# Layer 2 of a two-layer selective-scan kernel: the first group's preparation written as one ordered list, with x_proj of the second and third group moved into the first group

## The chip, the cores and the metric

The kernel runs on one core of a Trainium2 chip, as one launch. The metric is the device time of that launch in microseconds. Five engines work side by side, each with its own instruction queue that it takes in order: TensorE (PE), VectorE (DVE), ScalarE (ACT), GpSimd (POOL), and SyncE (SP), which here only issues DMAs. Semaphores make one engine wait for another. [...]

## What is computed

Two layers, each a residual block on a 64 x 64 image with 96 channels: group norm, an input projection to 192 channels and a gate, a 3 x 3 depthwise convolution with SiLU, four directional state-space scans, a layer norm, the gate, and an output projection. The change is in the scans of the second layer:

```python
xs = jnp.stack([xf, xf[:, :, ::-1], xf[:, :, o1], xf[:, :, o2]], axis=1)
x_dbl = jnp.einsum('bkdl,kcd->bkcl', xs, x_proj_weight)          # x_proj
dts = jnp.einsum('bkrl,kdr->bkdl', x_dbl[:, :, :DT_RANK], dt_projs_weight)
Bs = x_dbl[:, :, DT_RANK:DT_RANK + D_STATE]
Cs = x_dbl[:, :, DT_RANK + D_STATE:]
A = -jnp.exp(A_logs)
# selective_scan, for each of the 4096 positions t:
delta = softplus(dts + dt_projs_bias)
h = h * exp(delta_t * A) + (delta_t * u_t) * B_t                 # 192 channels x 16 states
y = sum over states of h * C_t                                   # + u * D
```

## The kernel before

**Groups and units.** Layer 2's scans (function `scans`, lines 654 to 1040) are cut into 16 groups: two kinds of path, two directions each, four chunks of 1024 positions (`TC`) each. The 192 channels are three tiles T of 64; the two halves of the 128 partitions hold an even and an odd state, so that 16 states are 8 pairs m (`NP`). One unit is one (T, m): a tile of 128 partitions by 1024 positions. A group has 24 units (`PER`), the whole layer 384. The order within a group goes by twos: T = 0 with m = 0 and 1, T = 1 with m = 0 and 1, T = 2, then m = 2 and 3, and so on.

**What one unit does.** `stage_a`: ACT makes the decay a = exp(dt * A). The input b comes in two ways. For an even unit, `stage_B` has PE spread the row of B over the partitions (bank pair b0), and DVE multiplies it by du in `stage_b`. For an odd unit, ACT has made products bT of the transposed du and a column of B (`product`), and `stage_t` has PE transpose eight of them into bank pair b1; no DVE multiplication is needed. `stage_s`: DVE's scan h = a * h + b, which needs the end of the previous group's scan of that unit (`carry`). `stage_c`: POOL multiplies h by C (tile cb, fetched from DRAM by `fetch_c` on SP's queue, three buffers). `stage_r`: PE folds the two states and adds into the banks y0, y1, y2; the first unit of a T begins its bank with a matmul of y. PSUM has eight banks: b0 and b1 two each, y0 to y2, and one named v.

**The preparation of a group** (`prelude`, from line 714). `project` has PE compute x_proj (pj) in two halves of 512 positions, three matmuls each; `projected` copies it to xd (one buffer) on ACT. `first_part`, `less_part`, `next_part` split B into three bfloat16 pieces: ACT casts a piece, PE subtracts it in pj (weights `less`), ACT casts the next, and so twice. `rows` writes C to DRAM. `tokens_B` transposes B on PE, `tokens_B_out` copies it to BT on ACT. `delta(T)` is softplus with a correction for what is lost in 1 + w: PE computes pd (`begin`); ACT does Abs, Relu, Exp, Ln and Identity; DVE does the `missed` step (w); and three two-operand steps (ln, sp, su: `found`, `whole`, `times`) follow on POOL, or on DVE for group 0. `spread(T)` copies sp to dt and su to du, onto both partition halves, by eight DMAs on SP's queue. `tokens_du` transposes su on PE, `tokens_du_out` copies it to duT on ACT. Sixteen `product` operations on ACT then make the bT of two m.

**What sets the order.** Each step of a preparation has a slot, counted in units from the start of the previous group, so that a group is prepared while the one before it scans. A main loop over j issues one round of stages for unit j and then the steps whose slots have come. Steps with a slot below 0 (all of group 0's preparation, and x_proj and the first pd of group 1) are issued before the loop. Up to j = 0 a scheduler may move instructions within a queue; from j = 0 on every instruction is held in program order, by these lines:

```python
def issue(*args, **more):
    ins = op(*args, **more)
    return tc.keep_in_program_order(ins) if pinned else ins
```

All instructions issued through this class have one line number in the profile, 670, and are told apart by their tiles. Group 0's preparation uses the banks y0, y1 for pj and y2, b1, v for pd; every later group uses v for everything.

Of the kernel before, what the change touches and what calls it, by code (L numbers as in the profile page):

```python
# [8 lines left out]
F32 = mybir.dt.float32  # L9
# [34 lines left out]
def two_ss2d_layers(  # L44
# [609 lines left out]
    def scans(weights):  # L654
# [2 lines left out]


        xw, dwb, _ = weights
        pinned = []  # L660

        class Ordered:
            def __init__(self, engine):
                self.engine = engine
# [1 line left out]
            def __getattr__(self, name):  # L666
                op = getattr(self.engine, name)

                def issue(*args, **more):
                    ins = op(*args, **more)  # L670
                    return tc.keep_in_program_order(ins) if pinned else ins

                return issue

        pe, act, dve, pool, sp = (
            Ordered(e) for e in (nc.tensor, nc.scalar, nc.vector, nc.gpsimd, nc.sync)
# [1 line left out]
        with ExitStack() as sc:  # L678
# [2 lines left out]
            pps = sc.enter_context(tc.tile_pool(name="pps", bufs=1, space=PSUM))  # L681
            dram = sc.enter_context(tc.tile_pool(name="dram", bufs=3, space=DRAM))
            load_exp_ln()
            am = decays(weights[2])
            carry = pre.tile([128, 3, NP], F32, name="carry")
            PER = 3 * NP
            LAG = 3
# [6 lines left out]
            def spare(name, tag="v"):  # L694

                if tag[0] == "b":
                    return pps.tile([128, TC], F32, tag=tag, name=name)[:, 0:HT]
                return pps.tile([128, HT], F32, tag=tag, name=name)
# [12 lines left out]
            def chunk(t, c):  # L711
                return t[:, HT * c : HT * (c + 1)]

            def prelude(k):


                p, d, c = GROUPS[k]
                me = state[k]
                add_engine = pool if k else dve

                tags = ("y0", "y1", "y2", "b1", "v") if k == 0 else ("v",) * 5

# [39 lines left out]

                def tokens_B():

                    ps = me["ps"] = spare(f"tB{k}")
                    for q in range(8):
                        pe.transpose(
                            ps[:, 32 * q : 32 * (q + 1)],
                            xd[0:32, 128 * q : 128 * (q + 1)], ident[0:32, 0:32],
                        )  # L770
# [8 lines left out]

                def tokens_du(e):  # L780

                    ps = me["ps"] = spare(f"tu{k}_{e}")
                    for T in range(3):
                        pe.transpose(
                            ps[:, 128 * T : 128 * (T + 1)],
                            me["su", T][:, 128 * e : 128 * (e + 1)], ident,
                        )

                def tokens_du_out(e):
                    t = me["duT", e] = pre.tile(  # L790
                        [128, 2, 3, 64], F32, tag=f"duT{e}", name=f"duT{k}_{e}"
                    )
                    act.copy(t, me["ps"][:, 0:384].rearrange("p (b h c) -> p h b c", h=2, c=64))


                def delta(T):

                    def begin():
                        ps = me["pd", T] = spare(f"pd{k}_{T}", tags[2 + T])
                        for h, half in enumerate(HALF):  # L800
                            pe.matmul(
                                ps[half], dwb[p][96 : NC + 1, d, T, half],
                                xd[96 : NC + 1, halves[h]], start=True, stop=True,
                            )

                    def new(nm, own):
                        t = me[nm, T] = pre.tile(
                            [128, HT], F32, tag=f"{nm}{T}" if own else nm, name=f"{nm}{k}_{T}"
                        )
                        return t  # L810

                    def absolute():
                        act.activation(new("su", True), me["pd", T], AF.Abs)

                    def positive():
                        act.activation(new("sp", True), me["pd", T], AF.Relu)

                    def exponent():
                        act.activation(new("w", False), me["su", T], AF.Exp, scale=-1.0)

                    def logarithm():
                        act.activation(new("ln", False), me["w", T], AF.Ln, bias=one)

                    def plus():
                        act.activation(me["pd", T], me["w", T], AF.Identity, bias=one)

                    def missed():

                        dve.scalar_tensor_tensor(
                            me["w", T], me.pop(("pd", T)), -1.0, me["w", T], ALU.add, ALU.subtract  # L830
                        )

                    def found():
                        add_engine.tensor_sub(me["ln", T], me["ln", T], me["w", T])

                    def whole():
                        add_engine.tensor_add(me["sp", T], me["sp", T], me["ln", T])

                    def times():
                        add_engine.tensor_mul(me["su", T], me["sp", T], chunk(u[T], c))  # L840

                    return [
                        begin, absolute, positive, exponent, logarithm, plus, missed,
                        found, whole, times,
                    ]

                def spread(T):
                    for nm, of in (("dt", "sp"), ("du", "su")):
                        t = me[nm, T] = pre.tile(
                            [128, TC], F32, tag=f"{nm}{T}", name=f"{nm}{k}_{T}"  # L850
                        )
                        both(t.rearrange("p (h t) -> p h t", h=2), me[of, T], sp)

                steps = []
                if (p, d) == (1, 0):
                    steps += [(-17 + T, lambda T=T: turn(T)) for T in range(3)]
                for h in range(2):
                    o = -13 + 3 * h

                    late = 0 if k else 9.5  # L860
                    steps += [
                        (o, lambda h=h: project(h)),
                        (o + 1, lambda h=h: projected(h)),
                        (o + 1 + late, lambda h=h: first_part(h)),
                        (o + 1 + late, lambda h=h: less_part(h)),
                        (o + 2 + late, lambda h=h: next_part(0, h)),
                        (o + 2 + late, lambda h=h: less_part(h)),
                        (o + 3 + late, lambda h=h: next_part(1, h)),
                    ]
                steps += [  # L870
                    (-9, rows), (-6.8, tokens_B), (-5.95, tokens_B_out),

                    *zip((-1.5, -1, -1, 0, 1, 1, 2, 3, 4, 5), delta(0)),
                    *zip((2.5, 3, 3, 4, 5, 5, 6, 7, 8, 9), delta(1)),
                    *zip((6.5, 7, 7, 8, 9, 9, 10, 11, 12, 13), delta(2)),
                ]
                steps += [(18.5 + e, lambda e=e: tokens_du(e)) for e in range(4)]
                steps += [(19 + e, lambda e=e: tokens_du_out(e)) for e in range(4)]
                steps += [(18 + 2 * T, lambda T=T: spread(T)) for T in range(3)]


                turns = (
                    (19, (4, 4, 4, 4)), (PER, (3, 1, 5, 1, 3, 3)), (PER + 6, (4, 2, 3, 1, 3, 3)),
                    (PER + 12, (2, 3, 3, 2, 3, 3)),
                )
                for i, (slot, counts) in enumerate(turns):
                    todo = [(e, h, n) for e in range(4) for h in range(2) for n in range(2)]
                    for s, count in enumerate(counts):
                        steps += [
                            (slot + s + 0.1, lambda i=i, at=at: product(k, i, *at))  # L890
                            for at in todo[:count]
                        ]
                        del todo[:count]
                return steps

            def product(k, i, e, h, n):


                me = state[k]
                if (h, n) == (0, 0):  # L900
                    me["bT", i, e] = mn.tile(
                        [128, 2, 3, 2, 64], F32, tag="bT", name=f"bT{k}_{i}{e}", bufs=7
                    )
                q = 2 * (2 * i + 1) + n
                act.mul(
                    me["bT", i, e][:, h, :, n, :], me["duT", e][:, h],
                    me["BT"][:, e + 4 * h, q : q + 1],
                )
# [90 lines left out]
            def stage_y(j):  # L999
# [6 lines left out]
                        act.copy(view, f(ps))  # L1006

            steps = [
                (PER * (k - 1) + slot, n, step, k)
                for k in range(len(GROUPS)) for n, (slot, step) in enumerate(prelude(k))  # L1010
            ]

            steps.sort(key=lambda at: (at[0] >= 0, at[0] < 0 and at[3], at[:2]))
            while steps[0][0] < 0:
                steps.pop(0)[2]()

            def unit(step, at):
                if 0 <= at < N:
                    step(at)

            for j in range(-5, N + LAG + 2):
                if j == 0:
                    pinned.append(True)

                for ahead, odd in ((4, 0), (1, 1)):
                    k, i = divmod(j + ahead, PER)
# [353 lines left out]
```

## Time and profile before

| | us |
|---|---|
| median of 3 runs | 1559.88 (1557.27 to 1559.94) |
| profiled execution, time | 1555.25 |
| its span, first to last instruction | 1553.5 |
| busy: PE / DVE / ACT / POOL | 1256.0 / 1350.1 / 1203.1 / 1093.8 |
| x_proj of layer 2's group 0 begins | 288.96 |
| first scan of group 0 / first DVE multiplication of group 1 | 314.31 / 412.51 |
| one scan of 128 x 1024 (xcount 288 and 96) | 2.34 and 2.28 |
| one DVE multiplication of 128 x 1024 | 1.21 |
| mean granted TensorE clock over the span | 0.91 |

Times in the profile are microseconds from the span's start. A row of a timeline gives the start, the duration, the engine, the line, the operation, the tile written and the tiles read (buffer numbers left out), the shapes, and how many such instructions are merged into the row; in brackets stands how long the engine was idle before it and whose instruction ended that. "PE b" means that a matmul that writes tile b was the last to come. Clock 0.50 is half of TensorE's full clock. A PE row counts the two passes of a 32-bit matmul as two instructions. The time of a run is a little longer than the span, 1555.25 against 1553.5.

### The profile page before, as it was taken

The page shows a single profiled execution, that of the slowest core. Times are in us where ns is not written, and L with a number is a line of the kernel's source. Part 1 is how long each engine was busy: PE and PEld are TensorE (multiplying, and loading weights), DVE is VectorE, ACT ScalarE, POOL GpSimd, SP SyncE. Part 2 cuts the span into 40 slices and gives each one's busy share as a digit, 9 for nine tenths or more (in the row PEclk, how much of TensorE's full clock was granted, in tenths as well). Part 3 has the DMA queues.
Part 4 walks back from the last instruction along what each step waited for, and adds up shares of the span by engine and source line. Part 5 has one row for each costly group of instructions (what it writes and reads, how often), then busy time and mean ns, then how long its engine had stood idle before and what let it go on. Part 6 is the DMA issues. An engine that isn't in the chain of part 4 may idle for free.

```text
span 1553.5 us, 17352 instructions
## 1 busy us (share of the span) xinstructions
PE 1256.0 (81%) x5158; PEld 504.4 (32%) x5158; DVE 1350.1 (87%) x932; ACT 1203.1 (77%) x2476; POOL 1093.8 (70%) x577
## 2 busy tenths in 40 slices
PE   5954779769888979887888889797978888876778
PEld 3433424223233323332333333333333332322223
DVE  6836489339999999999999999999999999999976
ACT  3445134759999898989999999999898989987733
POOL 0032000019898989899998989898989999998750
PEclk8975689759999999999989999999999899999999
DMA  4031320432626263544526262526263443626233
GB/s 110 20 107 35 105 71 1 134 73 55 138 57 136 64 145 80 123 100 92 134 68 151 59 138 56 136 57 149 68 138 82 110 110 82 136 62 152 60 93 83
DMA packets 83059, 146.33 MB, mean 94 GB/s; under 512 B 31580, under 2 KB 33820, under 8 KB 82860
## 3 DMA queue, kind: packets, MB, share of 16 engines
q1 hardware_dynamic: 80844, 144.35, 38.4%
q10 hardware_dynamic: 2112, 0.79, 0.2%
q8 instruction: 42, 0.69, 0.2%
q14 instruction: 61, 0.50, 0.1%
HBM read 80.85 MB, written 12.13 MB: 60 GB/s over the span
## 4 chain that ended last, share of the span: by engine, by line
DVE 28%; issue 22%; PE 13%; ACT 10%; POOL 5%; DMA 5%; SPq 4%; DVEq 0%; POOLq 0%; ACTq 0%
DVE h L670 18%; DVE b L670 7%; POOL hc L670 4%; SPq L670 4%; ACT a L670 3%; PE ys L670 3%; DMA cb<-C 3%; PE b L670 2%; PE cp L1137 2%; ACT bT L670 2%; PE pj L670 2%; PE pd L670 1%; DVE w L670 1%; PE in L1084 1%; PE m L1205 1%
## 5 line engine op out<-in xcount | busy, mean ns | idle before, releaser
L670 POOL TENSOR_TENSOR hc<-h,cb 128x1024 f32<-128x1024 f32 x384 | 902.8, 2368 | 204.1 <-DMA dt<-sp 95.5
L670 DVE TENSOR_TENSOR_SCAN h<-a,carry,b 128x1024 f32<-128x1024 f32 x288 | 665.1, 2337 | 27.0 <-PE b L670 5.6
L670 ACT ACTIVATE a<-dt,am 128x1024 f32<-128x1024 f32 x384 | 438.6, 1143 | 92.3 <-DVE h L670 90.6
L670 PE MATMUL ys<-hc,fold 128*64 128x512 f32 x1536 | 429.4, 639 | 3.5 <-POOL hc L670 3.5
L670 ACT ACTIVATE bT<-duT,BT 128x192 f32<-128x192 f32 x1024 | 391.6, 445 | 5.1 <-PE b L670 3.0
L670 PE MATMUL b<-ident,bT 128*128 128x128 f32 x1536 | 222.0, 287 | 33.8 <-DVE h L670 27.6
L670 DVE TENSOR_TENSOR b<-b,du 128x1024 f32<-128x1024 f32 x192 | 232.0, 1208 | 3.5 <-PE b L670 3.2
L670 DVE TENSOR_TENSOR_SCAN h<-a,b 128x1024 f32<-128x1024 f32 x96 | 216.0, 2277 | 20.2 <-PE b L670 12.9
L670 PEld LDWEIGHTS b<-ident,bT 128*128 128x128 f32 x1536 | 174.2, 146 | 158.7 <-DVE h L670 99.7
L670 PE MATMUL b<-B,selh 96*128 96x512 bf16 x384 | 122.2, 401 | 96.1 <-DVE h L670 95.4
L670 PEld LDWEIGHTS ys<-hc,fold 128*64 128x64 f32 x1536 | 78.5, 139 | 140.8 <-issue 97.5
L670 PE MATMUL pd<-xd,dwb 29*64 29x512 f32 x192 | 60.3, 693 | 53.7 <-DVE w L670 46.9
L670 PEld LDWEIGHTS <-selh 96*128 96x128 bf16 x384 | 26.1, 98 | 222.5 <-DVE h L670 126.8
L670 PE MATMUL pj<-u,xw 64*124 64x512 f32 x192 | 94.2, 636 | 2.4 <-ACT sz L1119 1.7
L1160 DVE SCALAR_TENSOR_TENSOR acc<-pad,v,acc 128x1052 f32<-128x1052 f32 x64 | 79.6, 1308 | 0.2
L670 POOL TENSOR_TENSOR ln<-ln,w 128x512 f32<-128x512 f32 x45 | 57.6, 1279 | 14.8 <-DVE w L670 14.8
L670 PE MATMUL ys<-y,ident 128*128 128x512 f32 (+1 forms) x120 | 63.3, 634 | 0.0
L1137 PE MATMUL cp<-pad,diag 128*128 128x512 f32 x144 | 62.3, 593 | 0.0
L670 ACT CAST B<-pj 96x512 bf16<-96x512 f32 (+2 forms) x96 | 55.1, 575 | 6.4 <-PE pj L670 6.3
L670 POOL TENSOR_TENSOR sp<-sp,ln 128x512 f32<-128x512 f32 x45 | 57.5, 1278 | 0.0
L670 DVE SCALAR_TENSOR_TENSOR w<-pd,w 128x512 f32<-128x512 f32 x48 | 32.1, 668 | 29.2 <-ACT pd L670 28.6
L670 POOL TENSOR_TENSOR su<-sp,u 128x512 f32<-128x512 f32 x45 | 57.3, 1274 | 0.0
(164 smaller groups left out, 1142.2 us busy)
## 6 DMA issues: line engine op xcount, KB each, us to landing
cb<-C SPq DMA_DIRECT2D x256, 256.0 KB, 4.1
dt<-sp SPq DMA_DIRECT2D x192, 128.0 KB, 4.3
du<-su SPq DMA_DIRECT2D x192, 128.0 KB, 3.9
szd<-sz SPq DMA_DIRECT2D x24, 256.0 KB, 3.1
szt<-szd SPq DMA_DIRECT2D x24, 256.0 KB, 6.5
xT<-xs SPq DMA_DIRECT2D x8, 384.0 KB
xs<-xT SPq DMA_DIRECT2D x1, 1536.0 KB
xs<-xT SPq DMA_DIRECT2D x8, 192.0 KB, 2.3
```

What stands on the lines that cost most here:

```text
L670: ins = op(*args, **more)
L1084: nc.tensor.matmul(ps[half], ipw_s[:, 64 * b : 64 * b + 64], xn[:, g * 512 : (g + 1) * 512], start=True, stop=True,)
L1137: nc.tensor.matmul(ps.rearrange("p (r w) -> p r w", w=HW), diag[:, k, :], pad[b][:, c, i : i + SR, j : j + HW], start=(k == 0), stop=(k == ...
L1160: nc.vector.scalar_tensor_tensor(acc, src, wk, acc, ALU.mult, ALU.add)
L1205: nc.tensor.matmul(pm, pos, y[T][:, cut], start=(T == 0), stop=(T == 2))
```

## The change

Only `scans` changes. Five things are done.

1. Every instruction of `scans` is now held in program order, also those before the loop; the loop begins at j = 0. Steps before it are no longer sorted and issued from slots.
2. Group 0's preparation is a new function, `first`, a list of calls. It has x_proj of both halves, xd, C, then pd of all three T, tB, then for each T the softplus on ACT (`by_scalar`), the rest on DVE (`by_vector`) and the spreading, with the decays' constants (am) placed within T = 1. The decay of unit 0 is next, then the bfloat16 pieces, the transposes of su with their copies, the first 16 products, stage B of unit 0 and the decay of unit 1.
3. Work of group 0 is shared: dt is copied by SP's queue and du by POOL's; two of the four duT copies go to DVE; of the first 16 products four stay on ACT, eight go to DVE, four to POOL. Relu is gone for group 0: DVE takes the maximum with 0 and adds in one operation. The transposes of du go to four different banks.
4. Group 1's preparation gets slots within group 0: x_proj from slot 0 to 4, its delta from slot 4.5 on.
5. Group 2's x_proj moves from slots -13 to -7 to slots -10.8 to -7, counted from its own start.

```diff
-                steps = []
+                def by_scalar():
+                    t = mn.tile([128, TC], F32, tag="hc", name=f"wl{T}", bufs=4)
+                    w, ln = me["wl", T] = t[:, halves[0]], t[:, halves[1]]
...
+                    act.activation(w, me["pd", T], AF.Abs)
+                    act.activation(w, w, AF.Exp, scale=-1.0)
+                    act.activation(w1, w, AF.Identity, bias=one)
+                    act.activation(ln, w, AF.Ln, bias=one)
+                def by_vector():
+                    w, ln = me["wl", T]
+                    dve.scalar_tensor_tensor(w, me["w1", T], -1.0, w, ALU.add, ALU.subtract)
+                    dve.tensor_sub(ln, ln, w)
+                    dve.scalar_tensor_tensor(new("sp", True), me["pd", T], 0.0, ln, ALU.max, ALU.add)
+                    dve.tensor_mul(new("su", True), me["sp", T], chunk(u[T], c))
...
-                        both(t.rearrange("p (h t) -> p h t", h=2), me[of, T], sp)
+                        queue = sp if k or nm == "dt" else pool
+                        both(t.rearrange("p (h t) -> p h t", h=2), me[of, T], queue)
...
+                at = {
+                    1: ((0, 1, 1.2, 2), (2, 3, 3.2, 4), 3, 4.1, 4.3),
+                    2: ((-10.8, -10, -9.4, -9), (-9, -8, -7.4, -7), -8, -6.8, -5.95),
+                }.get(k, ((-13, -12, -11, -10), (-10, -9, -8, -7), -9, -6.8, -5.95))
...
+                for T in range(3):
+                    o, slots = 4 * T, (-1.5, -1, -1, 0, 1, 1, 2, 3, 4, 5)
+                    if k == 1:
+                        o, slots = 3 * T, (4.5, 5, 5, 6, 6, 6, 7, 8, 8.5 + T // 2, 9 + T // 2)
+                    steps += zip((o + slot for slot in slots), delta(T))
...
+            def first(...):
+                parts = [delta(T) for T in range(3)]
+                for h in range(2):
+                    project(h)
+                for h in range(2):
+                    projected(h)
+                rows()
+                for begin, by_scalar, by_vector in parts:
+                    begin()
+                tokens_B()
+                for T, (begin, by_scalar, by_vector) in enumerate(parts):
+                    by_scalar()
+                    if T == 1:
+                        tokens_B_out()
+                        am.extend(decays(weights[2]))
+                    by_vector()
+                    spread(T)
+                    if T < 2:
+                        fetch_c(0, T)
+                stage_a(0)
+                for h in range(2):
+                    first_part(h)
+                for h in range(2):
+                    less_part(h)
+                for h in range(2):
+                    next_part(0, h)
+                for h in range(2):
+                    less_part(h)
+                for e in range(4):
+                    tokens_du(e)
+                for e in (0, 2, 1, 3):
+                    tokens_du_out(e)
+                for h in range(2):
+                    next_part(1, h)
+                for e, engine in enumerate((act, dve, dve, pool)):
+                    for h in range(2):
+                        for n in range(2):
+                            product(0, 0, e, h, n, engine)
+                stage_B(0)
+                stage_a(1)
```

## The prediction

> **What bounds the kernel now.** I began with the whole page: VectorE (DVE) is busy 87% of the span, and in section 2 its digit is 9 in every slice of layer 2 but the first two. So I cut those two apart by stretches of time (length; busy time of each engine with its instruction count; granted TensorE clock; DMA share; GB/s), with a whole later group of 73 us as yardstick.
>
> ```profile
> core 0: us, PE busy (x) PEld busy (x) DVE busy (x) ACT busy (x) POOL busy (x), PEclk, DMA share, GB/s
> 302.00:314.00 12.00, 2.20 (x6) 0.47 (x3) 8.03 (x12) 8.61 (x14) 0.00 (x0) 0.50 0.72 156
> 314.00:326.00 12.00, 10.33 (x21) 4.37 (x21) 2.50 (x2) 8.11 (x21) 2.36 (x1) 0.50 0.77 172
> 326.00:338.00 12.00, 9.96 (x21) 4.49 (x21) 5.70 (x3) 3.12 (x6) 4.70 (x2) 0.50 0.00 0
> 338.00:350.00 12.00, 4.33 (x16) 1.50 (x17) 0.88 (x2) 7.44 (x16) 0.11 (x1) 0.50 0.03 5
> 350.00:362.00 12.00, 12.00 (x42) 4.05 (x44) 9.83 (x6) 12.00 (x28) 10.14 (x6) 0.74 0.13 37
> 402.00:475.00 73.00, 61.27 (x277) 23.18 (x275) 70.83 (x41) 67.18 (x145) 67.75 (x34) 0.98 0.44 104
> ```
>
> In a later group DVE works 70.8 of 73 us: there DVE alone is the bound, and nothing in the change touches it. Between 302 and 350 it works 17 of 48 us. Next the timeline of DVE (start, duration, instruction, idle time before it and what ended it):
>
> ```profile
> 314.31 2.29 DVE L670 TENSOR_TENSOR_SCAN h<-a,b 128x1024 f32<-128x1024 f32 x1
> 326.91 2.29 DVE L670 TENSOR_TENSOR_SCAN h<-a,b 128x1024 f32<-128x1024 f32 x1 [10.32 <-PE b L670]
> 329.12 1.21 DVE L670 TENSOR_TENSOR b<-b,du 128x1024 f32<-128x1024 f32 x1
> 330.43 2.29 DVE L670 TENSOR_TENSOR_SCAN h<-a,b 128x1024 f32<-128x1024 f32 x1
> 349.12 0.69 DVE L670 SCALAR_TENSOR_TENSOR w<-pd,w 128x512 f32<-128x512 f32 x1 [16.41 <-ACT pd L670]
> 349.73 2.28 DVE L670 TENSOR_TENSOR_SCAN h<-a,b 128x1024 f32<-128x1024 f32 x1
> 352.84 1.23 DVE L670 TENSOR_TENSOR b<-b,du 128x1024 f32<-128x1024 f32 x1 [0.83 <-PE b L670]
> ```
>
> Units 0 to 3 scan at 314.31, 326.91, 330.43, 349.73. Two holes, 10.3 and 16.4 us. The first ends with transposed products (PE b), the second with w of the *second* group, which in queue order stands before unit 3's scan: its x_proj (pj) runs on PE, then delta, while DVE waits. The third view is PE's timeline; it shows why pj is so long:
>
> ```profile
> 320.78 5.48 PE L670 MATMUL pj<-u,xw 64*124 64x512 f32 x6
> ...
> 331.58 5.48 PE L670 MATMUL pj<-u,xw 64*124 64x512 f32 x6
> ...
> 377.04 2.84 PE L670 MATMUL pj<-u,xw 64*124 64x512 f32 x6
> ```
>
> The same half projection costs 5.48 us at clock 0.50 and 2.84 at full clock.
>
> **The change, part by part.** All times below are of the profiled execution (1555.25 us, span 1553.5).
>
> *1. Up to xd: nothing.* pj of group 0 runs at 288.96 as before, xd is complete at 293.4. The four am activations (1.03 us) leave their place ahead of xd, but xd's first half waited for pj anyway.
>
> *2. Delta of group 0.* pd_0 is no longer mixed with less-part and tB matmuls: ends about 294.6 (a pd is 1.07 us warm, 1.97 cold). ACT: Abs, Exp, Identity, Ln, one on the other, 0.60 to 0.66 each by the rows at 308, so 2.5: 297.1. Relu goes (3 x 0.49 us of ACT), max joins the DVE operation. DVE's four steps stay at 0.73 apart: sp_0 at 299.4, su_0 at 300.1. For T=1 ACT is done at 299.7, but DVE must first take the am scalings, whose ACT source is now behind Ln 1 and the BT copy: 301.0, four scalings, 301.5. DVE then does T=1 to 304.4, T=2 to 307.3 (before: 312.9).
>
> *3. Queues.* SP issued dt and du in turn, 24 issues at 0.595 us; now it has dt and two more cb fetches, and POOL has the twelve du. dt_0 is issued from 299.4, its fourth at 301.2, and lands, by the page's
>
> ```profile
> dt<-sp SPq DMA_DIRECT2D x192, 128.0 KB, 4.3
> du<-su SPq DMA_DIRECT2D x192, 128.0 KB, 3.9
> ```
>
> at 305.5. POOL has no DMA of its own in this trace. [...] I take 1.0, near SP's row: 12 us in all, partly waiting for su_2, over by 312.4. du_0 is wanted by the first multiplication at 316.8, so it is hidden.
>
> *4. A new wait.* ACT's decay a(0) stands in the list ahead of the B casts and waits for dt_0 until 305.5. Behind it: a 1.05, two casts 1.0, a less matmul (0.6), cast, less: 309.7. The tu transposes stand behind the less on PE, though su_2 is there at 307.3: this wait costs 2.4 us. Four tu at 0.9: 313.3, duT_3 on DVE 313.9.
>
> *5. First 16 products.* Before: 16 on ACT at 0.37 us in a chain with duT, 314.15 to 322.2. Now 4 on ACT, 8 on DVE, 4 on POOL, side by side. The shape 128x192 on DVE or POOL is not in the trace. DVE: between am's 0.19 us (48 elements) and w's 0.69 (512), so 0.36; range 0.2 to 0.5. POOL: 0.5 from its 1.28 for 512. DVE is last: 313.9 + 8 x 0.36 = 316.8. They stand ahead of the first multiplication, so **scan 0 is later than before: 318.1 against 314.3**. But scan 1 follows at once at 320.4, since its transposes end near 317. The 10.3 us hole is gone.
>
> *6. x_proj of group 1 inside group 0.* It is now spread between the units; does the stall go or only split up? PE, in order: t1, pj half, B2, less, less, t3, pj half, B4, ys. Cold durations from the rows: pj 5.41, t 1.96, B 0.97, less 0.6, ys of a new bank with its first pair 3.6.
> - pj 317.3 to 322.7, B2 323.7; DVE was free at 322.6: **1.2 lost**, scan 2 at 325.1.
> - less, cast, less, t3 end 327.7: 0.4 lost, scan 3 at 327.8.
> - second pj 327.7 to 333.1, B4 334.1; DVE free at 330.0: **4.2 lost**, multiplication 4 at 334.2.
> - ys to 337.7, two less with a cast between, t5 to 341.5; scan 4 ended 337.7: **3.8 lost**.
> - ys, tB, pd_0, B6 to 346.5 with the clock rising; DVE free at 343.8: **2.8 lost**. Then PE is ahead; multiplication 8 at 352.5.
>
> Before, multiplication 4 was at 352.84 and 8 at 366.09. So 13.6 us are won at unit 8.
>
> *7. Behind unit 8.* Group 1's w steps (0.6 us of DVE each) now lie at units 7, 10, 13, not 2, 6, 10: two more behind this point, -1.2. The third group's projection starts when w_2 frees bank v, one unit before its own transposes are needed: pj 2.84 + t 1.02 against multiplication and scan 3.6: -0.5. ACT has one more projection in group 0 (8 copies, 4 us) on 67.2 of 73, less 1.5 of y copies a first group lacks: 69.7 against DVE's 70.5. It is hidden, barely. From group 1 on all is as before, moved.
>
> Sum: 13.6 - 1.2 - 0.5 = **12 us**. 1555.25 - 12 = 1543 for a run like the profiled one; the median of the runs shown is 1559.88, so on its scale **1548**.
>
> [...] The row 314 to 326 disagrees: PE 10.3 of 12 us busy, clock 0.50, and so to 350, though pj alone is 5.4 us unbroken. The order after the change has the same mix (t, pj, B, less) up to the first ys, and before it was with ys that the clock rose. [...] I take the row.
>
> [...]
>
> **Rivals.**
> - A, clock opens early (in or before the first pj). For: [...]PE is denser from 309 on than before. Against: the row. Multiplication 8 at 342, saving 22: **1538**.
> - B, ACT or the single bank v holds group 0 back: pj, tB, pd and tu all pass through v, each waits for an ACT copy, and ACT is 99% full. For: ACT 67.2 of 73. Against: DVE's losses in step 6 give ACT time. About 5 us more lost: **1553**.
> - C, slower: POOL's twelve issues. The last four products stand behind them on POOL's queue, t1 and everything after behind those. With c us each they begin at 300.1 + 12c rather than 313.9: at 2.15 us all 12 us are lost[...]. For: no row shows the price. Against: SP's 0.6, and twelve issues of only 64 rows.
> - D, stall only moves: units 0 to 3 as slow as before. Against: the operations that filled 338 to 350 now stand behind unit 4. 1560.
>
> **Chances.** My forecast 0.50 (own range 1543 to 1552), A 0.22, B 0.17, C 0.07 with 1 in 4 of it still faster, D 0.04. Range 1537 to 1555: it takes in A's centre and B, leaves C, D and the far side of A. Faster by over 0.2% (3.1 us, what a measurement here can tell from nothing): 0.88; within 0.05; slower 0.07.
>
> **What would show it.** Step 4: ACT idle before a(0), ended by a dt landing near 305. Step 5: scan 0 near 318, scan 1 right behind. Step 6: DVE holes ended by PE b, none by ACT pd, before units 2, 4, 5, 6; pj at 5.4 us means the forecast, at 2.84 rival A. Step 3: POOL's last du issue before 314, else C. Wrong altogether if group 1's first multiplication (412.51 now) comes later than 408 or before 395.

## The result and the profile after

| | before | after |
|---|---|---|
| median of 20 runs each, side by side on one chip | 1559.57 us (1554.24 to 1571.26) | 1551.34 us (1543.67 to 1556.34) |
| profiled execution, its span | 1555.25, 1553.5 | 1545.96, 1543.8 |
| first DVE multiplication of group 0 / unit 4 / unit 8 | 312.99 / 352.84 / 366.09 | 315.77 / 333.52 / 349.22 |
| first multiplication of group 1 / last one of all | 412.51 / 1494.83 | 399.24 / 1487.61 |

The ratio is 0.9931, with a 95% interval from 0.9911 to 0.9951: **faster by 0.7%**, 8.2 us between the medians and 10.8 us by the ratio. The 20 runs of the kernel after fall into two clusters, nine of 1543.7 to 1547.5 us and eleven of 1551.1 to 1556.3, so that the median lies at the edge of the upper one and the profiled execution in the lower. The third and fourth line are from the two profiles, and they hold a puzzle. Group 1 begins 13.3 us earlier; at the last multiplication only 7.2 us of that are left.

The stretches of the kernel after, cut as before (length; busy PE, PEld, DVE, ACT, POOL; clock; DMA share; GB/s):

```profile
302.00:314.00 12.00, 5.71 (x19) 3.29 (x18) 7.36 (x14) 8.52 (x17) 6.79 (x13) 0.55 1.00 250
314.00:326.00 12.00, 10.02 (x21) 4.14 (x22) 9.94 (x11) 7.85 (x15) 7.13 (x6) 0.60 0.53 138
326.00:338.00 12.00, 11.36 (x21) 3.76 (x20) 6.84 (x4) 5.26 (x13) 5.38 (x3) 0.55 0.03 5
338.00:350.00 12.00, 11.43 (x57) 4.52 (x56) 9.26 (x6) 11.62 (x26) 7.37 (x4) 1.00 0.31 87
350.00:362.00 12.00, 8.99 (x44) 3.02 (x40) 11.77 (x8) 11.91 (x26) 11.92 (x7) 0.95 0.00 1
402.00:475.00 73.00, 63.59 (x270) 24.42 (x270) 69.45 (x40) 65.21 (x142) 66.11 (x33) 0.93 0.43 105
```

DVE's second to fourth row were 2.5, 5.7 and 0.9 us of 12; they are 9.9, 6.8 and 9.3. In the middle row PE was busy 11.4 us where it had been 10.0, and its clock there is still near half. The last row is worth a second look: in the same 73 us, where the change touches nothing, the clock is 0.93 where it was 0.98, and DVE does 69.45 us of work, not 70.83.

The timeline of DVE in the kernel after:

```profile
313.21 2.64 DVE L668 TENSOR_SCALAR bT<-duT,BT 128x192 f32<-128x192 f32 x8
...
317.03 4.46 DVE L668 TENSOR_TENSOR_SCAN h<-a,b 128x1024 f32<-128x1024 f32 x2
323.41 1.23 DVE L668 TENSOR_TENSOR b<-b,du 128x1024 f32<-128x1024 f32 x1 [1.92 <-PE b L668]
...
333.52 1.23 DVE L668 TENSOR_TENSOR b<-b,du 128x1024 f32<-128x1024 f32 x1 [3.99 <-PE b L668]
...
339.41 2.29 DVE L668 TENSOR_TENSOR_SCAN h<-a,b 128x1024 f32<-128x1024 f32 x1 [2.24 <-PE b L668]
342.89 1.23 DVE L668 TENSOR_TENSOR b<-b,du 128x1024 f32<-128x1024 f32 x1 [1.20 <-PE b L668]
```

The eight products of DVE come ahead of scan 0. Scans 0 and 1 are one row of two: the second follows at once. The holes of 10.3 and 16.4 us are replaced by 1.92, 3.99, 2.24 and 1.20 (and one of 0.21), all ended by PE b; no w of the second group waits for ACT. The PE rows of group 1's x_proj say why there are still holes:

```profile
316.93 5.48 PE L668 MATMUL pj<-u,xw 64*124 64x512 f32 x6
...
327.04 5.48 PE L668 MATMUL pj<-u,xw 64*124 64x512 f32 x6
```

Both halves ran at half clock, 5.48 and not 2.84 us. (The clock had been full from 312.9 to 316.3 and fell just ahead of the first.) ACT shows the new wait, and POOL its issues and products:

```profile
306.15 1.15 ACT L668 ACTIVATE a<-dt,am 128x1024 f32<-128x1024 f32 x1 [1.75 <-DMA dt<-sp]
```

```profile
301.90 2.27 POOL L668 DMA_DIRECT2D du<-su  x4 [79.75 <-ACT am L226]
...
308.18 2.08 POOL L668 DMA_DIRECT2D du<-su  x4 [0.81 <-DVE su L668]
313.48 2.99 POOL L668 TENSOR_SCALAR bT<-duT,BT 128x192 f32<-128x192 f32 x4 [3.21 <-DMA dt<-sp]
```

Four issues in 2.08 us are 0.52 us each, and all are over at 310.3, three microseconds ahead of the products.

### The profile page after: what moved, and what is told of

Same layout as the page of the kernel before. It is cut to its first block, busy times and chain, and to the rows that moved or that the text cites. A ratio compares the mean times of both kernels' runs of the same rounds, so it can differ in the third digit from the quotient of the medians.

```text
span 1543.8 us, 17370 instructions
## 1 busy us (share of the span) xinstructions
PE 1258.3 (82%) x5158; PEld 507.0 (33%) x5158; DVE 1354.3 (88%) x942; ACT 1196.7 (78%) x2459; POOL 1102.9 (71%) x593
## 3 DMA queue, kind: packets, MB, share of 16 engines
q1 hardware_dynamic: 79884, 142.78, 38.2%
## 4 chain that ended last, share of the span: by engine, by line
DVE 26%; issue 21%; PE 13%; ACT 11%; POOL 7%; DMA 6%; SPq 5%; DVEq 0%; POOLq 0%; ACTq 0%
DVE h L668 17%; DVE b L668 6%; POOL hc L668 5%; SPq L668 5%; ACT a L668 4%; PE ys L668 3%; ACT bT L668 2%; PE pj L668 2%; PE b L668 2%; PE cp L1216 2%; DMA cb<-C 2%; DMA du<-su 2%; DMA xT<-xs 1%; PE pd L668 1%; PE in L1163 1%
## 5 line engine op out<-in xcount | busy, mean ns | idle before, releaser
L668 PE MATMUL ys<-hc,fold 128*64 128x512 f32 x1536 | 434.2, 645 | 2.6 <-POOL hc L668 2.6
L668 ACT ACTIVATE bT<-duT,BT 128x192 f32<-128x192 f32 x1012 | 387.2, 445 | 8.3 <-PE b L668 6.4
L668 POOL DMA_DIRECT2D du<-su x12 | 6.4, 538 | 81.7 <-ACT am L226 79.7
```

Source lines behind the costliest of these rows:

```text
L668: return lambda *args, **more: tc.keep_in_program_order(op(*args, **more))
```

## The experiments

**How they are compared.** The profiles hold chance of two kinds. Group 0's own x_proj took 3.80 us in 11 of the 14 profiles and 7.13 to 7.17 in three, by the clock it met. And the later groups, which are the same in all kernels but the last three of the table, took between 1082 and 1092 us from group 1's first multiplication to the last one. So each kernel is judged by two numbers from its profile, the time from the end of group 0's x_proj to group 1's first multiplication ("to group 1") and from there to the last multiplication ("later groups"), beside the ratio of its runs to the kernel before on the same chip. Two profiles of one kernel agreed within 0.1 us to group 1 (before) and 0.7 us (after). The intervals of the ratios are 5 to 16 us wide, so the effects of 1.5 to 4 us below rest on one profile of each kernel and not on the ratios.

| kernel | to unit 4 | to group 1 | later groups | ratio (95%) |
|---|---|---|---|---|
| before | 60.1 | 119.75 | 1082.3 | 1 |
| before, second profile | 59.3 | 119.7 | 1084.5 | 1.0003 (0.9980 to 1.0025) |
| after | 39.8 | 105.5 | 1088.4 | 0.9931 (0.9911 to 0.9951) |
| after, second profile | 39.1 | 104.8 | 1091.9 | 0.9897 (0.9847 to 0.9947) |
| list alone | 49.2 | 109.5 | 1087.7 | 0.9937 (0.9910 to 0.9965) |
| slots alone | 45.5 | 111.4 | 1086.1 | 0.9970 (0.9953 to 0.9988) |
| five warming matmuls | 42.9 | 108.7 | 1091.1 | 0.9922 (0.9891 to 0.9953) |
| group 1's x_proj on 128 rows | 37.1 | 101.2 | 1085.9 | 0.9907 (0.9883 to 0.9930) |
| decay 0 behind the casts | 37.4 | 103.0 | 1090.7 | 0.9887 (0.9862 to 0.9912) |
| 16 first products on ACT | 41.1 | 107.0 | 1089.5 | 0.9922 (0.9897 to 0.9946) |
| du on SP's queue | 38.2 | 105.0 | 1088.9 | 0.9897 (0.9853 to 0.9942) |
| before, pd on 125 rows | 57.2 | 116.6 | 1075.6 | 0.9925 (0.9901 to 0.9949) |
| after, pd on 125 rows | 39.7 | 105.5 | 1076.1 | 0.9865 (0.9814 to 0.9915) |
| three edits together | 35.1 | 105.3 | 1074.2 | 0.9807 (0.9758 to 0.9856) |

So the change wins 14.3 us up to group 1, more than the 13.3 of the table in the section on the result because its profile's x_proj began 1 us later.

**1. The list alone, and the slots alone.** In the first the ordered list stays, and x_proj of groups 1 and 2 and group 1's delta have their old slots, those below 0 issued ahead of the loop:

```diff
-                    1: ((0, 1, 1.2, 2), (2, 3, 3.2, 4), 3, 4.1, 4.3),
-                    2: ((-10.8, -10, -9.4, -9), (-9, -8, -7.4, -7), -8, -6.8, -5.95),
...
+            while steps[0][0] < 0:
+                steps.pop(0)[2]()
```

> The ordered list for group 0 stays; group 1 has its old slots again (x_proj and first pd ahead of unit 1) and group 2 its old ones. Forecast's theory (the 16 us hole goes because group 1's x_proj leaves the front of the queues): scan 0 stays near 317, scan 1 waits for some 20 us of cold TensorE work and comes at 334 to 340, group 1's first multiplication at 403 to 406, time 0.995 to 0.997 of before. Rival (the list with its shared work brings nearly all): group 1 by 401, 0.993. Rival (it brings nothing): group 1 at 410 or later, 0.999 to 1.001.

The second is the kernel before with just those two lines of slots and group 1's slots of delta.

> The kernel before with the new slots of groups 1 and 2 alone; group 0's preparation and its 16 products on ScalarE as before. Forecast's theory: scan 0 at 314 to 315, scan 1 at 322 to 324 (products end at 322), then the same cold x_proj between the units; group 1's first multiplication at 401 to 404, time 0.994 to 0.995. Rival (slots only move the stall): group 1 at 409 or later.

Each alone wins a part: 10.2 and 8.3 us to group 1, where both win 14.3. The list's ratio (0.9937) is better than its forecast; the slots' (0.9970) is worse, and so is the time of their group 1, 409.2, in an execution in which group 0's x_proj ended 5 us later than before. By the runs the list alone is not to be told from the whole change (0.9931 and 0.9897); what the slots add to it, 4.0 us to group 1, is seen in the profiles alone. The timelines of DVE show where they overlap. In the list alone scan 1 comes this late:

```profile
333.42 2.29 DVE L668 TENSOR_TENSOR_SCAN h<-a,b 128x1024 f32<-128x1024 f32 x1 [14.21 <-PE b L668]
```

and in the slots alone:

```profile
326.86 2.29 DVE L670 TENSOR_TENSOR_SCAN h<-a,b 128x1024 f32<-128x1024 f32 x1 [6.19 <-PE b L670]
333.23 1.23 DVE L670 TENSOR_TENSOR b<-b,du 128x1024 f32<-128x1024 f32 x1 [4.09 <-PE b L670]
```

With the old slots, group 1's whole x_proj is ahead of unit 1's transposes in PE's queue, so the first products being early helps nothing until both halves are through: one hole of 14.2 us. With the new slots alone that hole is split, but the products still come late from ACT. The two parts work on the same hole.

**2. Does a warm clock cure the holes?** Five extra matmuls on all 128 rows behind tB, into the unused half of its bank pair (`me_full[0]` is the whole tile):

```diff
                 tokens_B()
+                for q in range(5):
+                    pe.matmul(me_full[0][:, HT:TC], ident, u[q % 3][:, 0:HT], start=True, stop=True)
```

> The changed kernel with five extra matmuls of 128x128 by 128x512 on TensorE behind the transposes of B, into an unused bank, while TensorE has nothing to do (299.5 to 307.8). Forecast's theory (holes before units 2, 4, 5 and 6, 9.6 us together, come from the half clock, and full-array work opens the clock where x_proj does not): clock 1.00 from about 306 on, x_proj of group 1 at 2.84 us a half in place of 5.48, the holes 2 to 4 us together, group 1 at 392 to 395, time 0.988 to 0.990 of before. Rival R (the clock opens and falls again at the first x_proj): second half still 5.4, 0 to 3 us won. Rival S (the holes are waits for the casts on ScalarE and the single bank v): the clock is 1.00 and 7 us or more of holes remain.

The windows of this kernel:

```profile
302.00:314.00 12.00, 6.38 (x20) 3.55 (x19) 6.11 (x12) 7.73 (x17) 5.01 (x11) 0.76 0.79 194
314.00:326.00 12.00, 10.51 (x23) 3.76 (x22) 9.82 (x14) 8.08 (x16) 7.68 (x7) 0.64 0.78 173
```

The clock was up for part of the time, from 301.5 to 308.3 and from 315.2 to 318.6 by its records. It fell there, just ahead of x_proj (318.98), and both halves again took 5.48 us, as rival R said. The edit also had a fault: tB's copy on ACT waited for the extra matmuls, since they write the same tile (4.92 us, until 304.47), and group 1 came 3.2 us later. So warming beforehand isn't shown to be worthless: the clock had fallen before x_proj began, and stayed at half through it.

**3. Rows.** That left a question: in the kernel after, PE was busy 11.4 of the 12 us from 326 to 338, and the clock stayed at half until 336.8. Group 1's x_proj reads 64 rows (one half of the partitions). Here its weights are put into tiles with zeros in the other 64 rows, and the matmuls read all 128: same result, same columns streamed.

```diff
+                        rows = slice(0, 128) if k == 1 else HALF[h]
+                        weight = wide_w[h][:, T, :] if k == 1 else xw[p][HALF[h], d, T, :]
                         pe.matmul(
-                            ps[0:NC], xw[p][HALF[h], d, T, :], chunk(u[T], c)[HALF[h]],
+                            ps[0:NC], weight, chunk(u[T], c)[rows],
```

> The kernel after, with group 1's x_proj matmuls on all 128 rows instead of 64: the weights of the other half's rows are zero, so the result is the same; streamed elements and duration per matmul at a given clock are the same. Theory (the clock stays at 0.50 in 314 to 336 because the half-row matmuls, t and B count for too little, not because PE has gaps): the clock opens in or right behind the first half of group 1's x_proj, the second half takes 2.84 us instead of 5.48, the holes of DVE before units 4, 5 and 6 shrink from 4.0, 2.3 and 1.2 us, and from the end of group 0's x_proj to group 1's first multiplication takes about 101 us instead of 105.5; ratio to the kernel before about 0.003 lower than that of the kernel after. Rival (rows make no difference, what counts is gaps or the whole stretch): both halves 5.48 again, 105 us, same ratio as after.

The PE rows of this kernel's x_proj:

```profile
318.07 4.86 PE L668 MATMUL pj<-u,wide_w 128*124 128x512 f32 x6
...
326.73 2.84 PE L668 MATMUL pj<-u,wide_w 128*124 128x512 f32 x6 [0.35 <-ACT B L668]
```

The clock opened inside the first half, at 322.3, and the second took 2.84 us. In all seven profiles of the list with the new slots and 64 rows the second half took 5.48. In the last experiment below, where the same 128-row matmuls ran again, the halves took 4.16 and 4.54: opened, but not held. DVE's holes before units 2, 4, 5 and 6 became 0.73, 0.84, 0.58 and 1.20. To group 1 it takes 101.2 us, where the theory said 101 and the rival 105. **So here the clock went with the rows that the matmuls feed, 64 or 128, and not only with how long PE was busy.** At full clock a half takes 2.84 us on either.

The other traces say the same. In the traces of before and after all 134 records of the clock begin at whole multiples of 3.413 us from the first one, so I cut all 14 profiles, from 296 us to 1490, into windows of that grid, and gave each the share of it that PE was busy, every matmul weighted by its rows out of 128 (an estimate, since the profile models the ends of matmuls). The bins below are my own. In 367 windows at half clock PE was busy for 99% or more of the time. Of those with a weighted share above 0.9 all 244 were followed by full clock, of those under 0.7 none of 78, of those between 24 of 45 (in before and after alone 36 of 36, none of 10, 4 of 6). In the kernel after, three windows of x_proj were full and weighted 0.55 to 0.58, and the clock stayed; the next, full of ys matmuls on 128 rows, had 0.99, and the clock opened at 336.8. In the other direction, all 172 windows at full clock with a weighted share under 0.4 were followed by half clock, and 4 of 3221 from 0.6 on (in before and after alone 21 of 21, and 1 of 436).

**4. The wait on dt.** The decay of unit 0 behind ACT's casts:

```diff
-                stage_a(0)
                 for h in range(2):
                     first_part(h)
...
                     next_part(0, h)
+                stage_a(0)
```

> The kernel after, with the decay of unit 0 put behind ACT's casts of the bfloat16 pieces instead of ahead of them. Theory (step 4 of the prediction: the decay waits for dt_0 until 306.15 and the casts, the less matmuls and the transposes of su wait behind it): ACT's wait on dt goes, the su transposes begin about 2 us earlier (when su_2 is there, 307.3 to 308), scan 0 is at about 315 instead of 317, and from the end of group 0's x_proj to group 1's first multiplication takes about 103.5 us instead of 105.5. Rival (su_2 or PE is what comes last anyway): less than 0.7 us earlier.

ACT no longer waits for dt:

```profile
305.17 1.06 ACT L668 CAST B<-pj 64x512 bf16<-64x512 f32 x2 [0.19 <-PE pj L668]
306.13 1.15 ACT L668 ACTIVATE a<-dt,am 128x1024 f32<-128x1024 f32 x1
```

103.0 us, 2.5 less than after. The new wait that the prediction priced at 2.4 us was real, and could be had back by moving one line.

**5. The first 16 products.** All on ACT again: `for e, engine in enumerate((act, act, act, act))`.

> The kernel after, with all 16 of the first products on ACT, as they were before the change, instead of 4 on ACT, 8 on DVE and 4 on POOL. Theory (step 5: sharing them is what lets scan 1 follow scan 0 at once): DVE is free of 2.6 us, so scan 0 comes 2 to 2.6 us earlier (about 314.5), but ACT makes the products until about 319 and scan 1 waits for its transposes: a hole of about 4 to 5 us before scan 1, and group 1's first multiplication 2 to 3 us later, about 108 us from the end of group 0's x_proj instead of 105.5. Rival (the sharing is worth nothing, since DVE then waits for PE at units 2, 4, 5 anyway): 105 to 106.

Between the two expectations: 107.0 us. Scan 0 came at 314.07, 3 us earlier, for DVE had no products to make. Scan 1 then waited for something else than expected, ACT's decay of unit 1, which stands behind the 16 products:

```profile
318.49 2.29 DVE L668 TENSOR_TENSOR_SCAN h<-a,b 128x1024 f32<-128x1024 f32 x1 [2.14 <-ACT a L668]
```

Sharing the products is worth 1.5 us here, twice what two profiles of one kernel differ by. The other 12.8 us belong to the rest of the change together; its shared duT copies and the missing Relu were not taken back one by one.

**6. The second queue.** du back on SP, behind dt: `queue = sp`.

> The kernel after with the copies of du back on SP's queue, behind those of dt, as before the change; POOL issues no DMA. Theory (step 3 of the prediction: the second queue is hidden, since du_0 is wanted only by the first multiplication): SP's 24 issues and the cb fetches end near 320 instead of 317; dt_1 is wanted by the decay of unit 2 at 319.4 and lands before it; scan 0 at 317 as in the kernel after, 105.5 us from the end of group 0's x_proj to group 1's first multiplication within 1 us, ratio as after. Rival (the second queue is what makes the early products possible): du_0 or dt_1 land late, DVE waits for a DMA before the first multiplication or ACT before the decay of unit 1 or 2, 2 to 5 us later. The other way round: du lands sooner from SP (3.9 us before the change against 6.8 from POOL), nothing waits for it, no gain.

No loss: 105.0 us. But dt_0 came sooner, and ACT hardly waited:

```profile
304.50 1.15 ACT L668 ACTIVATE a<-dt,am 128x1024 f32<-128x1024 f32 x1 [0.34 <-DMA dt<-sp]
```

From the first dt issue to this decay it is 4.3 us. In the kernels in which POOL copies du at the same time and the decay waits for dt, it is 5.1 to 5.7, and twice 7.7 to 7.8. That the two copies compete is the likely reason; nothing here separates it from another. (The two of 7.7 to 7.8 are the two kernels with the 128-row x_proj; why is open.) The 1.6 us that unit 4 is earlier are mostly lost again by group 1.

**7. Where 5 us went in the later groups.** The kernel before and after were each profiled again.

> The kernel before once more, for a second profile of it. Theory P (the 13.3 us won by group 1 and the 9.7 won over the span differ by chance: the groups behind group 1 have the same instructions in the same order, and their lengths go with where the clock's low stretches fall in each execution): in this profile, from group 1's first multiplication to the last one takes another time than the 1082.3 us of the first profile, anywhere between 1080 and 1092, and from the start of group 0's x_proj to group 1's first multiplication about 123 us. Rival Q (the change itself makes the later groups slower): 1082 again, within 1.5.

> The changed kernel itself, profiled a second time. From the first multiplication of group 1 to the last one of the layer it took 1082.3 us before the change and 1088.4 after, in one profile each, though the instructions there are the same and in the same order. Theory P (the granted TensorE clock dips at other places in each execution): group 1 begins again within 0.5 us of 399.2 counted the same way, but the later stretch comes out anywhere from 1081 to 1090, with single groups off by 1 to 2 us. Rival Q (the change itself lengthens the later groups): the stretch is again 1088 to 1089, group by group as in the first profile.

The second profile of before (1084.5) lies in P's range and just outside Q's; the second of after (1091.9) lies outside both. That execution was 8.7 us longer than the first: 3.3 in group 0's x_proj, 3.5 in the later groups, 2.3 behind the last multiplication. In six profiles of kernels with the list and the new slots, x_proj and pd unchanged, the later groups take 1088 to 1092 us, in two of before 1082 and 1084: more than I called chance. Low-clock records showed what to try. Half clock takes 113 and 109 us of the later groups in the two profiles of after, 92 and 96 in those of before. In the kernel after, a window of 3.4 us at full clock that is followed by half clock holds 0.52 us of pd, the others 0.09 (over all eleven profiles with the old pd 0.55 and 0.09, less apart than the 0.66 and 0.10 of the expectation below); pd feeds 29 rows. xd has 124 rows and one of ones, so with zeros in dwb's other rows pd can read all 125:

```diff
-            nc.vector.memset(v[96:128, 0:D], 0.0)
+            nc.vector.memset(v[:, 0:D], 0.0)
...
-                                ps[half], dwb[p][96 : NC + 1, d, T, half],
-                                xd[96 : NC + 1, halves[h]], start=True, stop=True,
+                                ps[half], dwb[p][0 : NC + 1, d, T, half],
+                                xd[0 : NC + 1, halves[h]], start=True, stop=True,
```

> The kernel before, with layer 2's pd matmuls on 125 rows instead of 29: the added rows of the weights are zero, so the result and the time per matmul at a given clock are the same. In the profiles so far, the stretch of 3.4 us ahead of a low-clock stretch in the later groups holds 0.66 us of pd against 0.10 elsewhere. Theory P (the later groups' lengths of 71.2 to 74.1 us come from the clock falling behind pd, at a phase that differs by chance): hardly any low clock behind group 1, every later group 71 to 72.5 us long, and so some 10 to 20 us less than the kernel before over groups 1 to 15. Rival (pd has nothing to do with it): low-clock time and lengths as before, ratio 1.000.

> The kernel after with the same edit. Theory P: with the chance of the clock's phase gone from the later groups, group 1's first multiplication to the last takes the same time, within 2 us, as in the kernel before with the edit, and the change's saving over the whole run equals what is won by group 1, 13 to 15 us: ratio to the kernel before lower by 0.0085 to 0.0095 than that of the kernel before with the edit. Rival Q (the change itself makes the later groups some 5 us slower, by something else than the clock): those 5 us remain, and the difference is 0.005 to 0.0065.

The same long stretch of the later groups in four kernels; first before, then after:

```profile
412.00:1475.00 1063.00, 891.74 (x3922) 343.47 (x3920) 1026.58 (x570) 956.90 (x2015) 975.75 (x478) 0.96 0.43 102
```

```profile
412.00:1475.00 1063.00, 895.94 (x3906) 343.88 (x3902) 1020.76 (x566) 948.76 (x1995) 972.08 (x477) 0.95 0.43 100
```

then before and after with pd on 125 rows:

```profile
412.00:1475.00 1063.00, 880.55 (x3941) 339.41 (x3940) 1032.41 (x573) 960.73 (x2022) 980.23 (x481) 0.97 0.44 102
```

```profile
412.00:1475.00 1063.00, 871.59 (x3941) 336.23 (x3940) 1031.87 (x573) 952.22 (x2000) 981.21 (x481) 0.98 0.43 101
```

DVE is the bound there, so its busy time is the progress made. After had done 5.8 us less than before in the same time, at clock 0.95 against 0.96: that is the loss. With pd on 125 rows both do more, and the same (1032.4 and 1031.9). The later groups take 1075.6 and 1076.1 us, and the change wins 11.2 us up to group 1 and 11.0 over the span: nothing is lost later. The first expectation had the direction right and the size wrong: the kernel before wins 6.7 to 8.9 us there and not 10 to 20, and 61 us at half clock are left. In these profiles, one of each kernel, the loss goes when pd's rows are filled, so it was one of TensorE's clock, and Q finds no support. The ratios of the two (0.9925 and 0.9865) can't decide: their difference of 0.006 lies in Q's range, not in P's, but has an interval of half 0.005 and more, and with 11 us won by group 1 even P comes to 0.007. What stays open is why the kernel after met a low clock for longer than before in every profile taken, with the same instructions in the same order. Time at half clock is not the whole measure either: with pd on 125 rows it is 61 us for before and 38 for after, at equal length. With the old pd a group's length went with where in the clock's grid of 3.413 us it began (last section), and the grid lay differently in the two executions: its boundaries come 1.28 us behind whole multiples of 3.413 us from the span's start in before, 2.28 in after.

**8. A faster version.** Edits 3, 4 and pd together.

> The kernel after with three edits: the decay of unit 0 behind the casts, group 1's x_proj matmuls on 128 rows, pd on 125 rows. If the three effects add up: group 1's first multiplication 98 to 99 us behind the end of group 0's x_proj instead of 105.5, the later groups as in the kernel after with pd on 125 rows, so 5 to 7 us less than that one. If they overlap (the earlier start meets the clock still low): 2 to 4 us less.

Median 1532.15 us (1528.28 to 1538.22), ratio 0.9807: **1.9% under the kernel before, and the lowest ratio of all**; against the kernel after with pd alone (0.9865) the median is 8.3 us lower, more than was expected, but the intervals overlap. Its profiled execution took 1538.22 us, 6.1 more than the median, and shows neither expectation met: unit 4 came 35.1 us after x_proj, the earliest of all, yet group 1 no earlier than after (105.3). ACT waited for dt three times, though the first decay now stood behind the casts:

```profile
312.54 1.15 ACT L668 ACTIVATE a<-dt,am 128x1024 f32<-128x1024 f32 x1 [1.63 <-DMA dt<-sp]
320.39 1.15 ACT L668 ACTIVATE a<-dt,am 128x1024 f32<-128x1024 f32 x1 [2.59 <-DMA dt<-sp]
326.41 1.15 ACT L668 ACTIVATE a<-dt,am 128x1024 f32<-128x1024 f32 x1 [0.71 <-DMA dt<-sp]
```

The x_proj of the third group, still on 64 rows, met a low clock in this execution:

```profile
365.69 5.17 PE L668 MATMUL pj<-u,xw 64*124 64x512 f32 x6 [1.14 <-DVE w L668]
```

and DVE had holes of 3.73, 2.22 and 2.37 us behind it. Weights on 128 rows for that group as well, and du back on SP's queue, were not tried together with these edits.

## Why the prediction was right, step by step

The forecast was 1548, the median is 1551.3, inside the range and, by 0.7 us, inside the forecast's own range of 1543 to 1552. The mechanism came as forecast up to group 1; that the sum came near was partly luck, as the last point says.

- **Step 1 was right** for what the change moves; that x_proj itself can take 3.8 or 7.1 us by the clock it meets was not seen, and adds chance of 3.4 us to any single profile.
- **Step 2 was right:** su_2 was done at 307.9, where 307.3 was said.
- **Step 3:** an issue on POOL took 0.51 to 0.57 us, not 1.0 (an estimate from SP's 0.595), and the last was over at 310.3, not 312.4. Rival C had set the point of no gain at 2.15; it falls. What an issue on POOL costs while DVE copies was not shown: DVE's copies began at 312.1, when the issues were over. But the queue isn't free: du landed 6.8 us after its issue (SP: 4.2), and dt, which is waited for, came later than in experiment 6.
- **Step 4 was right:** ACT waited for dt_0 until 306.15 (305.5), and experiment 4 puts the cost at 2.5 us (2.4).
- **Step 5:** DVE's products took 0.33 us (0.36), POOL's 0.75 (0.5); scan 0 at 317.03 (318.1), scan 1 right behind. Right, though experiment 5 shows that the sharing is the smaller part of it.
- **Step 6 was right in its kind and 2.8 us too dear.** Losses of 1.92, 0.21, 3.99, 2.24 and 1.20 against 1.2, 0.4, 4.2, 3.8 and 2.8. The terms before units 5 and 6 were mis-sized: the clock opened at 336.8, in the first ys matmuls, not step by step up to 346. Unit 8 at 349.22 (352.5). Counted from x_proj's end, 17.9 us are won there, where 13.6 were forecast. The choice of the row 314 to 326, clock 0.50, held: 5.48 us twice. Rival A's open clock did not come on 64 rows. In experiment 3, on 128 rows, it opened at 322.3, 4.2 us behind the start of x_proj.
- **Step 7 was too cheap:** 3.6 us behind unit 8, not 1.7. Of these, 2.67 are four small holes of DVE between 371 and 382, where 0.5 was forecast. Two, of 0.45 us, end with PE b, as the forecast had it; the larger two end with ACT's pieces of B for the third group:

```profile
371.68 2.29 DVE L668 TENSOR_TENSOR_SCAN h<-a,b 128x1024 f32<-128x1024 f32 x1 [0.52 <-ACT B L668]
379.31 2.29 DVE L668 TENSOR_TENSOR_SCAN h<-a,b 128x1024 f32<-128x1024 f32 x1 [1.25 <-ACT B L668]
```

That is rival B's wait in small: ACT was "hidden, barely", and here it was not. The list alone, which keeps the third group's old slots, has none of these holes and takes 46.4 us from unit 8 to group 1, as before; after takes 50.0 and the slots alone 50.8. So the new slots cost these 3.6 us. (Slots count from the start of the group before. The third group's x_proj thus lay within the first group before the change too, from unit 11 on; the change moves it to unit 13 there.)
- **What failed is the last sentence of step 7, "From group 1 on all is as before, moved".** 13.3 us were won at group 1, but the last multiplication is 7.2 us earlier and the span 9.7 shorter. From the sum of 12 to these 9.7: 4.3 us more won up to unit 8, 1.9 more lost behind it, 6.1 lost in the later groups, 2.4 won behind the last multiplication, and 1.0 lost by x_proj's later start. The last two are not the change's doing. The medians give 8.2. That the sum is near is therefore partly luck: an error of 4.3 us and two of 1.9 and 6.1 partly cancel.

## What to carry over

The ordered list paid here, where several engines' queues must meet at one point, and the parts of the change overlap: measure each alone before adding them up. In the list, look at each instruction that waits for a DMA and ask what stands behind it: moving one decay behind four casts gave 2.5 us. Where TensorE is busy but its clock is low, as here on 64 rows, count the rows its matmuls read; widening pd from 29 rows to 125 with zero weights gave about as much as the whole change (9.1 us between medians side by side).

## What the hardware showed

- In the kernel after TensorE's clock stayed at half from 316.3 to 336.8 with PE busy 11.4 of 12 us (326 to 338); in that stretch lie both halves of group 1's x_proj, 5.48 us each on 64 rows. With this x_proj on 128 rows the clock opened at 322.3, within the 4.9 us of the first half. pd on 125 rows rather than 29 made the kernel before faster by 0.75% (ratio 0.9925, 0.9901 to 0.9949) with no other edit.
- Two x_proj halves on the two halves of the rows, one issued behind the other, took 3.80 us in all in group 0 at full clock, in the profiles of before and after. One alone took 2.84 at full clock, on 64 rows or on 128. So the two overlapped by 1.88 us.
- The clock's records in the profiles of before and after, 62 and 72 of them, change on a grid of 3.413 us. Of the 154 later groups of the 11 profiles with the old pd, 40 began in the same 0.75 us of that grid, and 34 of these took 73.0 us, which no other group did; the groups altogether ranged from 71.2 to 78.3. DVE being their bound, their length here went with where the grid lay when they started.
- The products of 128 x 192 came every 0.33 us on DVE, 0.75 on POOL and 0.37 on ACT, the three side by side.
